# Score products of 64 rows with new turn orders, and strand work moved from VectorE to ScalarE and GpSimd

## The chip, the cores and the metric

One core of one Trainium2 chip. The metric is the device time of one launch in microseconds (us); the kernel before took 1256.9, 1262.49 and 1262.93 us in three runs, median 1262.49. A profile of one execution is given beside them. Engines: PE is TensorE (matrix products), PEld its weight loads, DVE is VectorE, ACT is ScalarE, POOL is GpSimd, SP the engine that issues most transfers.

## What is computed

A macaron block on x of 2 x 1024 tokens by 512 channels, in float32:

```python
x = x + 0.5 * ffn(layernorm(x))
x = x + attn(layernorm(x))
x = x + 0.5 * ffn(layernorm(x))

def ffn(x):            # 8 experts of rank 16, the two best of a softmax router
    h = einsum('td,erd->ter', x, lora_A)
    lora = einsum('ter,eor,te->to', h, lora_B, w_top2) * 2.0
    return x @ W_base.T + b_base + lora

def bitnet_linear(x, W, scale):
    s = maximum(mean(abs(W), axis=1), 1e-8)
    y = einsum('bsi,oi->bso', x, sign(W / s[:, None])) * (s * scale)
    return nan_to_num(y, nan=0.0, posinf=1e6, neginf=-1e6)

def attn(x):           # 32 query heads, 8 key/value heads, head width 16
    q, k, v = (bitnet_linear(x, W, sc) for W, sc in ((Wq, qs), (Wk, ks), (Wv, vs)))
    p = softmax(q @ k.T / 4)          # each key/value head serves 4 query heads
    return bitnet_linear(p @ v, Wo, os)
```

## The kernel before

**Layout.** Tokens are cut into tiles of 128; four tiles are a group, so there are groups (b, g) = (0,0), (0,1), (1,0), (1,1). PSUM has eight banks of 128 x 512: seven rotate under the tag `w` (`bank`), one holds the value sums `av`.

**Units and turns.** The attention works on 32 units: batch, block of 512 queries, key/value head. A unit has 4 query heads. `attention` (L831) runs a loop of turns. In one turn stand eight score tiles for the row maxima of one unit (`m_tile`, 128 queries by 512 keys), eight score tiles for the exponentials of an earlier unit (`e_tile`, 128 keys by 512 queries) and the value products (`a_part`) of what the turn before exponentiated. A unit takes four turns in each role.

**A score tile.** Queries and keys are held as a rounded high part and a low part, so that products in the reduced format (fp32r) keep the precision of float32. The tile `q` has 32 rows for each head: 16 high, 16 low; four heads fill 128 partitions. The tile `k` holds the high and the low keys side by side, repeated on every 16 rows. A product of 32 rows against the low keys and one against the high keys are summed in a bank (L742, L781). An exponential's tile gets a third product of 2 rows, which subtracts the row maximum (L785). A product of 32 rows uses a strip of 32 of TensorE's 128 rows; head h lies on strip h.

**After the product.** VectorE reduces each m tile to its negated maximum (`m_max`, L751); ScalarE exponentiates each e tile (L787). The value products (L820) use all 128 rows and 32 columns each, so that four heads lie side by side.

**Order.** All instructions are issued in an order written out by the program, and every engine works through its own in order. A turn follows one of three texts: `FULL` when a strand has a TensorE step ready, else `BARE`; `LEAD_IN` before the first exponentials. In them `m0(5)` and `m1(5)` are the two products of m tile 5, `e0(3)`, `e1(3)` and `e2(3)` the three of e tile 3, `A0` to `A3` the four quarters of the value products, `S` the placing of a unit's maxima; `F` offers one TensorE step to the strands, `V` one VectorE operation, `C` one ScalarE operation, `W` and `D` the same under a condition. Tile i belongs to head i mod 4.

**Strands.** Everything else (first FFN, projections, output projection, second FFN) is written as Python generators which the planner `Flow` runs beside the attention. A `yield "v", "P"` asks for a VectorE slot after a TensorE step; a table of delays (`LATER`) in planner ticks, 64 to a turn, says how long after a step the next may be issued. `flow.stock` counts buffers: `t` are the temporary 128 x 512 tiles. `flow.free` is true outside the attention. Where a unit needs projections that are not issued yet, `need` (L839) issues strand steps alone, ahead of the turn's further instructions, until they are; `place(u)` (L682) then loads a unit's q and k. Unit 16 is the first of batch 1; it is placed at the end of turn 60.

**Steps that the change touches.** `finite` (L226) is nan_to_num of four elementwise operations and a predicated copy; in strands beside the attention, three run on GpSimd and the mask (L251) and the copy (L259) on VectorE. `ln_T` normalizes a tile on VectorE (L288), transposes it on TensorE and copies it on ScalarE. `base` in the FFN forms x + b/2 in a new tile on GpSimd (L414) and adds the product on VectorE (L425). `o_proj` multiplies by the output scale on VectorE (L639). `qkv_part` stores the high and low parts of queries and keys to `qd` and `kd` in DRAM (L543).

## Time and profile before

| | us |
|---|---|
| median of three runs | 1262.49 |
| the profiled execution, its own time | 1256.92 |
| its span, first to last instruction | 1255.2 |
| TensorE busy | 1148.8 |
| VectorE busy (reductions of m tiles: 657.0) | 902.8 |
| ScalarE busy (exponentials: 546.9) | 641.6 |
| GpSimd busy | 295.0 |
| mean granted TensorE clock | 0.915 |

A busy engine is one that has an instruction in it; overlapping matrix products count once, and their ends are modelled. So the starts of products tell more than their lengths. Idle time of an engine that is not the bound costs nothing. The chain of work that ended last follows the time back from the last instruction, at each step to what released it. In a line of groups or of the timeline, `out<-in` are tile names without their numbers, and `32*128 32x512` is a product on 32 rows and 128 columns of the array over 512 moving columns. A matrix product in full float32 appears as two instructions.

### The profile page before, as it was taken

How to read it: one execution, taken by the hardware profiler on the slowest of the kernel's cores; microseconds unless marked ns; L12 is line 12 of the kernel's file. 1: busy time of each engine (PE TensorE's matmuls, PEld its weight loads, DVE VectorE, ACT ScalarE, POOL GpSimd, SP SyncE). 2: the span in 40 equal slices, each digit the busy share in tenths (PEclk: the TensorE clock that was granted, in tenths of full speed). 3: DMA queues.
4: the chain of work that ended last, by engine and by line, in shares of the span. 5: the costliest groups of instructions: out<-in, count | busy, mean ns of one | idle time of the engine just before them, and what ended most of it. 6: DMA issues, size and time to landing. Idle time of an engine off the chain costs nothing.

```text
span 1255.2 us, 25499 instructions
## 1 busy us (share of the span) xinstructions
PE 1148.8 (92%) x10501; PEld 606.1 (48%) x10501; DVE 902.8 (72%) x1733; ACT 641.6 (51%) x1249; POOL 295.0 (24%) x302
## 2 busy tenths in 40 slices
PE   3988699999999999999999999999999999998868
PEld 3546355454454544444554445444455444545434
DVE  5578876767786777776677976777769677895273
ACT  2222255655554665565565666455557655566401
POOL 3135832000000340031555220241000300422110
PEclk8989588899986999987999899899989899999788
DMA  7010332121212222223132241122222422211110
GB/s 254 1 59 34 81 122 85 52 52 52 52 52 52 69 80 57 70 76 89 49 90 75 72 122 53 33 52 69 61 60 67 123 68 65 68 55 38 45 39 34
DMA packets 38708, 85.57 MB, mean 68 GB/s; under 512 B 7728, under 2 KB 10800, under 8 KB 34624
## 3 DMA queue, kind: packets, MB, share of 16 engines
q1 hardware_dynamic: 37184, 81.26, 22.4%
q8 instruction: 82, 1.34, 0.4%
q10 hardware_dynamic: 1152, 2.10, 0.4%
q0 software_dynamic: 256, 0.59, 0.3%
q14 instruction: 34, 0.28, 0.1%
HBM read 59.57 MB, written 23.84 MB: 66 GB/s over the span
## 4 chain that ended last, share of the span: by engine, by line
PE 70%; DVE 19%; issue 3%; DMA 2%; POOL 2%; ACT 1%; SPq 1%; POOLq 0%; ACTq 0%; DVEq 0%
PE av L820 20%; PE m L742 16%; DVE mn L751 11%; PE e L781 10%; PE pbf L419 5%; PE pbs L419 5%; PE e L785 4%; PE po L634 2%; PE phs L342 1%; DMA qd<-y 1%; PE pq L504 1%; PE pbf L423 1%; PE pv L521 1%; PE pbs L423 1%; DMA x<-in_x 1%
## 5 line engine op out<-in xcount | busy, mean ns | idle before, releaser
L751 DVE TENSOR_REDUCE mn<-m 128x1 f32<-128x512 f32 x1024 | 657.0, 682 | 230.0 <-PE m L742 221.4
L787 ACT ACTIVATE es<-e 128x512 f32<-128x512 f32 x1024 | 546.9, 599 | 425.6 <-PE e L785 401.4
L742 PE MATMUL m<-k,q 32*128 32x512 f32 x2048 | 492.1, 464 | 21.1 <-DVE mn L751 15.1
L781 PE MATMUL e<-q,k 32*128 32x512 f32 x2048 | 407.9, 474 | 8.3 <-DVE mn L751 6.9
L742 PEld LDWEIGHTS m<-k,q 32*128 32x128 f32 x2048 | 240.8, 196 | 153.0 <-issue 67.4
L820 PE MATMUL av<-es,vaug 128*32 128x256 f32 x4096 | 290.3, 416 | 16.4 <-issue 10.3
L781 PEld LDWEIGHTS e<-q,k 32*128 32x128 f32 x2048 | 185.1, 194 | 114.7 <-DVE mn L751 69.6
L785 PE MATMUL e<-mq,ones_r 2*128 2x512 f32 x1024 | 233.0, 431 | 3.7 <-DMA mq<-mT 3.7
L820 PEld LDWEIGHTS av<-es,vaug 128*32 128x32 f32 x4096 | 121.5, 116 | 154.5 <-issue 103.8
L785 PEld LDWEIGHTS e<-mq,ones_r 2*128 2x128 f32 x1024 | 125.6, 196 | 25.1 <-issue 13.7
L419 PE MATMUL pbf<-wb,xTf 128*128 128x512 f32 x128 | 68.9, 653 | 1.3 <-DVE mn L751 1.3
L419 PE MATMUL pbs<-wb,xTs 128*128 128x512 f32 x128 | 64.8, 618 | 1.2 <-DVE mn L751 1.2
L586 POOL TENSOR_TENSOR an<-an,rb 128x512 f32<-128x512 f32 x15 | 19.2, 1281 | 142.7 <-DMA rd<-rs 72.1
L249 POOL TENSOR_SCALAR loa<-y 128x512 f32<-128x512 f32 x17 | 12.7, 750 | 157.1 <-ACT y L509 147.5
L726 POOL MEMSET vaug<- 128x128 f32 x32 | 6.6, 206 | 137.7 <-PE av L820 137.6
L419 PEld LDWEIGHTS pbf<-wb,xTf 128*128 128x128 f32 x128 | 23.2, 203 | 30.1 <-issue 26.1
L419 PEld LDWEIGHTS pbs<-wb,xTs 128*128 128x128 f32 x128 | 21.5, 189 | 27.1 <-issue 22.9
L253 POOL TENSOR_SCALAR z<-y 128x512 f32<-128x512 f32 x17 | 34.1, 2008 | 1.8 <-DMA qd<-y 0.6
L249 POOL TENSOR_SCALAR loo<-yo 128x512 f32<-128x512 f32 x12 | 7.4, 613 | 113.7 <-DVE yo L639 110.0
L537 POOL TENSOR_TENSOR z<-z,y 128x512 fp32r<-128x512 f32 x17 | 21.9, 1293 | 51.0 <-ACT y L534 51.0
L590 POOL TENSOR_TENSOR anxL<-an,anxT 128x512 fp32r<-128x512 f32 x15 | 19.2, 1280 | 53.5 <-ACT anxT L588 53.4
L634 PE MATMUL po<-sign_o,anxT 128*128 128x512 f32 x64 | 29.4, 459 | 1.2 <-DVE mn L751 1.2
(193 smaller groups left out, 1008.3 us busy)
## 6 DMA issues: line engine op xcount, KB each, us to landing
k<-kd SPq DMA_DIRECT2D x31, 1024.0 KB
q<-qd SPq DMA_DIRECT2D x32, 256.0 KB
ad<-avs SPq DMA_DIRECT2D x32, 256.0 KB
x<-in_x SPq DMA_DIRECT2D x16, 256.0 KB
qd<-y SPq DMA_DIRECT2D x16, 256.0 KB
qd<-z SPq DMA_DIRECT2D x16, 256.0 KB
an<-ad SPq DMA_DIRECT2D x15, 256.0 KB
rb<-rd SPq DMA_DIRECT2D x15, 256.0 KB
```

The source lines that it names most:

```text
L249: nc.gpsimd.tensor_scalar(lo_, y, 0.0, -BIG, ALU.min, ALU.max)
L253: nc.gpsimd.tensor_scalar(o, y, 0.0, BIG, ALU.max, ALU.min)
L419: nc.tensor.matmul(pb, xT[:, c, t * P:(t + 1) * P], wb[:, c, :], start=(c == 0), stop=False)
L423: nc.tensor.matmul(pb, hT[0][:, t * P:(t + 1) * P], lb, start=False, stop=True)
L537: (nc.vector if fast else nc.gpsimd).tensor_tensor(lo, o, y, ALU.subtract)
L634: nc.tensor.matmul(po, hs[j][:, c, t * P:(t + 1) * P], wo[:, c, :], start=(c + j == 0), stop=(c + j == KC))
L742: nc.tensor.matmul(s["m", i], s["q"][rows, qt * P:(qt + 1) * P], s["k"][rows, 1 - p, kh * 512:(kh + 1) * 512], start=(p == 0), stop=(p == 1))
L751: nc.vector.tensor_reduce(s["mn"][:, h, qt, kh:kh + 1], s.pop(("m", i)), AX.X, ALU.max, negate=True)
L781: nc.tensor.matmul(t, s["k"][rows, 1 - p, kt * P:(kt + 1) * P], s["q"][rows, :], start=(p == 0), stop=False)
L785: nc.tensor.matmul(t, ones_r[two, :], s["mq"][two, :], start=False, stop=True)
L787: nc.scalar.activation(e, s.pop(("e", i)), AF.Exp, scale=HD ** -0.5)
L820: nc.tensor.matmul(s["av"][32 * h:32 * h + 32, cols], s["v"][:, kt, :], s["es"][kt * REP + h][:, cols], start=(kt + half == 0), stop=(kt + ...
```

## The change

- The q and k of a unit now lie in one tile. The keys are stored as 64 rows for each key/value head (high twice, low twice) and loaded to both halves of the partitions; the queries' 32 rows are loaded twice, so that one product of 64 rows gives the whole score. An m tile takes one product instead of two, an e tile two (64 rows and 2 rows) instead of three. Heads 0 and 1 lie on partitions 0 to 63, heads 2 and 3 on 64 to 127.
- The three turn texts are new. `e1` is now the 2-row product. The choice between FULL and BARE looks ahead to the place of the first `F`.
- Before a unit's first value product, the planner now waits until the copy of the unit before has been issued.
- In strands beside the attention: the normalization runs on ScalarE with a bias that GpSimd computes; the mask of `finite` on GpSimd; the FFN's sum as a scaled copy on ScalarE and an addition on GpSimd; the output scale as a copy on ScalarE and a product on GpSimd. x + b/2 is formed in place. Outside the attention these stay on VectorE.
- 13 temporary tiles instead of 11 (stock 12 for 10).

```diff
     p2 = ctx.enter_context(tc.tile_pool(name="p2", bufs=2))
-    tmp = ctx.enter_context(tc.tile_pool(name="tmp", bufs=11))
+    tmp = ctx.enter_context(tc.tile_pool(name="tmp", bufs=13))
     sm = ctx.enter_context(tc.tile_pool(name="sm", bufs=4))
...
             self.t, self.free, self.strands, self.n = 0, True, [], 0
-            self.stock = dict(m=3, n=4, t=10, xT=2, xL=2, hT=1, fb=6)
+            self.stock = dict(m=3, n=4, t=12, xT=2, xL=2, hT=1, fb=6)
             self.lock = None
...
             nc.gpsimd.tensor_scalar(lo_, y, 0.0, -BIG, ALU.min, ALU.max)
-            yield "v", src, t
-            nc.vector.tensor_scalar(m_, y, 0.0, 0.0, ALU.mult, ALU.is_equal)
+            yield "g", ""
+            nc.gpsimd.tensor_scalar(m_, y, 0.0, 0.0, ALU.mult, ALU.is_equal)
             yield "g", ""
...
         nc.gpsimd.tensor_tensor(rstd[:, own], ve[:, own], mhalf[:, own], ALU.pow)
+        calm = not flow.free
+        if calm:
+            yield "g", ""
+            neg = sm.tile([P, TG], F32, tag="neg", name=f"neg{n}{tiles[0]}", bufs=4)
+            nc.gpsimd.tensor_tensor(neg[:, own], mv[:, own, 0], rstd[:, own], ALU.mult)
+            yield "g", ""
+            nc.gpsimd.tensor_scalar(neg[:, own], neg[:, own], -1.0, None, ALU.mult)
         at = flow.t
...
             yield "r", dict(t=1)
-            yield "v", "g", at
+            yield "a" if calm else "v", "g", at
             xn = t512(f"xn{n}_{t}")
-            nc.vector.tensor_scalar(xn, xt[:, t, :], mv[:, t, 0:1], rstd[:, t:t + 1], ALU.subtract,
-                                    ALU.mult)
-            yield "P", "v", None, 1
+            if calm:
+                nc.scalar.activation(xn, xt[:, t, :], AF.Identity, bias=neg[:, t:t + 1],
+                                     scale=rstd[:, t:t + 1])
+            else:
+                nc.vector.tensor_scalar(xn, xt[:, t, :], mv[:, t, 0:1], rstd[:, t:t + 1],
+                                        ALU.subtract, ALU.mult)
+            yield "P", "a" if calm else "v", None, 1
             pt = bank(f"pt{n}_{t}").rearrange("p (c q) -> p c q", c=KC)
...
             yield "g", ""
-            xb = t512(f"xb{n}_{t}")
-            nc.gpsimd.tensor_tensor(xb, xt[:, t, :], bh, ALU.add)
+            nc.gpsimd.tensor_tensor(xt[:, t, :], xt[:, t, :], bh, ALU.add)
             for c in range(KC):
...
             nc.tensor.matmul(pb, hT[0][:, t * P:(t + 1) * P], lb, start=False, stop=True)
-            yield "v", "P"
-            nc.vector.scalar_tensor_tensor(xt[:, t, :], pb, 0.5, xb, ALU.mult, ALU.add)
-            flow.give(t=1, fb=1)
+            if flow.free:
+                yield "v", "P"
+                nc.vector.scalar_tensor_tensor(xt[:, t, :], pb, 0.5, xt[:, t, :], ALU.mult, ALU.add)
+                flow.give(t=1, fb=1)
+            else:
+                yield "a", "P"
+                hb = t512(f"hb{n}_{t}")
+                nc.scalar.activation(hb, pb, AF.Copy, scale=0.5)
+                flow.give(fb=1)
+                yield "g", "a"
+                nc.gpsimd.tensor_tensor(xt[:, t, :], xt[:, t, :], hb, ALU.add)
+                flow.give(t=1)
             if store is not None:
-                yield ("a" if flow.free else "d"), "v"
+                yield ("a" if flow.free else "d"), "v" if flow.free else "g"
                 (nc.scalar if flow.free else nc.sync).dma_start(store[t * P:(t + 1) * P, :],
...
             if mv2 is not None:
-                yield "v", "v"
+                yield "v", "v" if flow.free else "g"
                 stats(xt, t, mv2, n)
...
             for j, t in enumerate((y, o)):
-                dst = (qd[b][i * 2 * P:(i + 1) * 2 * P, cols].rearrange(
-                           "(h i d) s -> h i d s", i=2, d=HD)[:, j, :, :] if i < KC
-                       else kd[b][:, j * S + g * GT:j * S + (g + 1) * GT])
-                yield ("d", "v" if fast else "g") if j == 0 else ("d", "d")
-                nc.sync.dma_start(dst, t)
+                n_ = 2 if i < KC else 4
+                dst = (qd[b][i * 2 * P:(i + 1) * 2 * P, cols] if i < KC else kd[b][:, cols]).rearrange(
+                    "(h i d) s -> h i d s", i=n_, d=HD)
+                for c in range(n_ // 2):
+                    yield ("d", "v" if fast else "g") if j + c == 0 else ("d", "d")
+                    nc.sync.dma_start(dst[:, j * n_ // 2 + c, :, :], t)
         flow.give(t=2 if i <= KC else 1)
...
                 flow.lock = ss[t] if c < 2 else None
-            yield "v", "P"
+            yield "v" if fast else "a", "P"
             y = t512(f"yo{n}_{t}")
-            nc.vector.tensor_tensor(y, po, osc, ALU.mult)
+            if fast:
+                nc.vector.tensor_tensor(y, po, osc, ALU.mult)
+            else:
+                nc.scalar.copy(y, po)
             flow.give(fb=1)
             done.append(t)
+            if not fast:
+                yield "g", "a"
+                nc.gpsimd.tensor_tensor(y, y, osc, ALU.mult)
             r = t512(f"ro{n}_{t}")
-            yield from finite(y[:, :], r[:, :], f"o{n}_{t}", fast, ("v", flow.t))
+            yield from finite(y[:, :], r[:, :], f"o{n}_{t}", fast, ("v" if fast else "g", flow.t))
             yield "v" if fast else "g", "v"
...
-    FULL = ("e0(3) e0(2) m0(5) m0(0) e1(3) e1(2) m1(5) V m1(0) e2(3) e2(2) C e0(1) A0 A1 A2 A3 S "
-            "m0(1) m0(6) e0(7) e0(4) m1(1) m1(6) e1(7) W e1(4) e1(1) m0(2) e2(7) e2(4) e2(1) C "
-            "m1(2) V F e0(6) e0(0) m0(7) e0(5) e1(6) e1(0) m1(7) e1(5) e2(6) e2(0) D m0(3) e2(5) "
-            "m0(4) m1(3) F m1(4)")
-    BARE = ("C m0(1) m0(2) e0(3) e0(4) V m1(1) e0(6) e1(3) e1(4) m0(5) e1(6) e2(4) e2(3) m1(5) "
-            "m1(2) A0 S e2(6) e0(1) m0(0) e0(7) e1(1) C m1(0) e1(7) W m0(6) e2(1) e0(0) e2(7) m1(6) "
-            "A1 e1(0) V m0(7) e0(5) e0(2) e2(0) D m1(7) e1(2) e1(5) m0(4) m0(3) e2(2) e2(5) m1(4) "
-            "m1(3) A2 A3")
-    LEAD_IN = ("m0(0) m0(5) m0(2) V m1(0) m1(5) F C V m0(7) m1(2) m1(7) V F C m0(4) m0(1) m0(6) V m1(4) "
-               "m1(1) F C V m0(3) V m1(6) S m1(3) F C V")
+    FULL = ("m0(5) V m0(3) C F F e0(4) m0(7) V W e0(1) e0(3) e1(1) e1(4) e0(2) e1(2) e1(3) m0(1) C "
+            "A0 A1 S e0(6) e0(0) e1(6) e0(5) m0(6) e1(0) e1(5) m0(2) D A2 A3 m0(4) e0(7) m0(0) "
+            "e1(7)")
+    BARE = ("e0(0) W m0(2) A0 S C e0(3) e1(0) e0(2) m0(4) e1(2) e1(3) m0(1) A1 A2 m0(0) C m0(7) "
+            "e0(1) e0(6) e0(4) e1(6) e1(4) D e1(1) m0(6) A3 m0(5) V e0(7) e0(5) m0(3) e1(5) e1(7) V")
+    LEAD_IN = ("m0(0) m0(5) m0(2) V m0(7) F C V m0(4) m0(1) V F C m0(6) V F C V m0(3) V S F C V")
     FULL, BARE, LEAD_IN = (
...
          for o in t.split()] for t in (FULL, BARE, LEAD_IN))
+    at_F = TICK * FULL.index(("F", 0, 0)) // len(FULL)
     TU = NT // 2
...
         b, qb, g = units[u]
-        q = p2.tile([P, 512], F32R, tag="q", name=f"q{u}", bufs=3)
-        nc.sync.dma_start(q.bitcast(F32), qd[b][g * P:(g + 1) * P, qb * 512:(qb + 1) * 512])
-        k = p2.tile([P, 2, S], F32R, tag="k", name=f"k{u}", bufs=3)
+        qk = p2.tile([P, 2, S], F32R, tag="k", name=f"k{u}", bufs=3)
+        q, k = qk[:, 0, :].rearrange("p (t s) -> p t s", t=2), qk[:, 1, :]
         st[u].update(q=q, k=k, es={}, mq=p2.tile([P, 512], F32R, tag="mq", name=f"mq{u}", bufs=3),
                      mn=p2.tile([P, REP, 4, 2], F32, tag="mn", name=f"mn{u}"))
+        for t in range(2):
+            for h in range(2):
+                row = g * P + (2 * h + t) * 32
+                nc.sync.dma_start(q.bitcast(F32)[64 * h:64 * h + 64, t, :],
+                                  qd[b][row:row + 32, qb * 512:(qb + 1) * 512].unsqueeze(0)
+                                  .to_broadcast([2, 32, 512]))
         if u:
-            nc.sync.dma_start(k.bitcast(F32).rearrange("p i s -> p (i s)"),
-                              kd[b][g * HD:(g + 1) * HD, :].unsqueeze(0).to_broadcast(
-                                  [P // HD, HD, 2 * S]))
-
-    def place_k(half):
-
-        for i in range(2):
-            nc.sync.dma_start(st[0]["k"].bitcast(F32)[:, i, half * 512:(half + 1) * 512],
-                              kd[0][0:HD, i * S + half * 512:i * S + (half + 1) * 512]
-                              .unsqueeze(0).to_broadcast([P // HD, HD, 512]))
+            place_k(u, 0, S)
+
+    def place_k(u, s0, s1):
+        b, _, g = units[u]
+        nc.sync.dma_start(st[u]["k"].bitcast(F32)[:, s0:s1],
+                          kd[b][g * 64:(g + 1) * 64, s0:s1].unsqueeze(0).to_broadcast(
+                              [2, 64, s1 - s0]))
...
         place(0)
-        place_k(0)
+        place_k(0, 0, 512)
         for j in range(4):
             yield "P", "d" if j == 0 else "", None, 4
-            for p in range(2):
-                for h in range(REP):
-                    m_tile(0, j * REP + h, p, False)
+            for h in range(REP):
+                m_tile(0, j * REP + h, False)
             for h in range(REP):
...
         yield "d", "x"
-        place_k(1)
+        place_k(0, 512, S)
...
-    def m_tile(u, i, p, end=True):
+    def rows_of(h):
+        return slice(64 * (h // 2), 64 * (h // 2) + 64)
+
+    def m_tile(u, i, end=True):
...
         h, (qt, kh) = i % REP, m_where(u, i)
-        rows = slice(32 * h, 32 * h + 32)
-        if p == 0:
-            s["m", i] = bank(f"m{u}_{i}")
-        nc.tensor.matmul(s["m", i], s["q"][rows, qt * P:(qt + 1) * P],
-                         s["k"][rows, 1 - p, kh * 512:(kh + 1) * 512],
-                         start=(p == 0), stop=(p == 1))
-        if p == 1 and end:
+        s["m", i] = bank(f"m{u}_{i}")
+        nc.tensor.matmul(s["m", i], s["q"][rows_of(h), h % 2, qt * P:(qt + 1) * P],
+                         s["k"][rows_of(h), kh * 512:(kh + 1) * 512], start=True, stop=True)
+        if end:
             m_max(u, i)
...
         kt, h = i // REP, i % REP
-        rows = slice(32 * h, 32 * h + 32)
         if p == 0:
-            s["e", i] = bank(f"e{u}_{i}")
-        t = s["e", i]
-        if p < 2:
-            nc.tensor.matmul(t, s["k"][rows, 1 - p, kt * P:(kt + 1) * P], s["q"][rows, :],
-                             start=(p == 0), stop=False)
+            t = s["e", i] = bank(f"e{u}_{i}")
+            nc.tensor.matmul(t, s["k"][rows_of(h), kt * P:(kt + 1) * P], s["q"][rows_of(h), h % 2, :],
+                             start=True, stop=False)
         else:
+            t = s["e", i]
             two = slice(32 * h, 32 * h + 2)
...
         def need(*keys):
+            until(lambda: set(keys) <= ended)
+
+        def until(cond):
             for _ in range(4000):
                 flow.settle()
-                if set(keys) <= ended:
+                if cond():
                     return
...
                 place_v(e[0])
-            order = (LEAD_IN if not e and not a else FULL if flow.wants("P", begin + TICK * 5 // 8)
+            order = (LEAD_IN if not e and not a else FULL if flow.wants("P", begin + at_F)
                      else BARE)
...
                     if m:
-                        m_tile(m[0], m[1] * 2 * REP + i, p)
+                        m_tile(m[0], m[1] * 2 * REP + i)
                 elif kind == "e":
...
                     if a:
+                        if a[0] and a[1] == p == 0:
+                            until(lambda: "av" not in st[a[0] - 1])
                         a_part(a[0], a[1] * 2 + p // 2, p % 2)
...
     qd = [dram.tile([2 * D, S], F32, tag="qd", name=f"qd{b}") for b in range(B)]
-    kd = [dram.tile([P, 2 * S], F32, tag="kd", name=f"kd{b}") for b in range(B)]
+    kd = [dram.tile([4 * P, S], F32, tag="kd", name=f"kd{b}") for b in range(B)]
     ad = [dram.tile([G * P, S], F32, tag="ad", name=f"ad{b}") for b in range(B)]
...
     rd = [dram.tile([NQB, H, 512], F32, tag="rd", name=f"rd{b}") for b in range(B)]

```

## The prediction

> **What bounds the kernel now.** I read the page first (engine totals, then the chain that ended last), then the waits, then stretches of the timeline of TensorE, VectorE and GpSimd inside the attention, and last the order of the instructions in the two programs.
>
> ```profile
> span 1255.2 us, 25499 instructions
> PE 1148.8 (92%) x10501; PEld 606.1 (48%) x10501; DVE 902.8 (72%) x1733; ACT 641.6 (51%) x1249; POOL 295.0 (24%) x302
> ...
> PE 70%; DVE 19%; issue 3%; DMA 2%; POOL 2%; ACT 1%; SPq 1%; POOLq 0%; ACTq 0%; DVEq 0%
> ```
>
> TensorE is the bound, VectorE the second. One full turn of the attention, from TensorE's timeline, with its columns start, length, engine, line, operation, tiles, shapes, count:
>
> ```profile
> 893.53 0.50 PE L742 MATMUL m<-k,q 32*128 32x512 f32 x2
> 893.54 0.49 PE L781 MATMUL e<-q,k 32*128 32x512 f32 x2
> 893.87 0.39 PE L742 MATMUL m<-k,q 32*128 32x512 f32 x1
> 893.87 0.39 PE L781 MATMUL e<-q,k 32*128 32x512 f32 x2
> 894.10 0.38 PE L781 MATMUL e<-q,k 32*128 32x512 f32 x1
> 894.11 0.40 PE L785 MATMUL e<-mq,ones_r 2*128 2x512 f32 x2
> 894.33 0.39 PE L785 MATMUL e<-mq,ones_r 2*128 2x512 f32 x1
> 894.66 1.13 PE L419 MATMUL pbs<-wb,xTs 128*128 128x512 f32 x2
> 895.71 0.50 PE L781 MATMUL e<-q,k 32*128 32x512 f32 x2
> ...
> 899.00 1.93 PE L820 MATMUL av<-es,vaug 128*32 128x256 f32 x32
> ```
>
> Starts are what counts. Four products on four different strips of 32 rows start within 0.01 us; the next four 0.23 us later (893.87, 894.10, 894.33). I call such a step a slot. Where the shape changes, a step is longer: 894.33 to 894.66 is 0.33 before the 128-row product, and the second slot after the change comes 0.34 after the first (893.53 to 893.87). So a change of shape costs about 0.1 on either side, 0.2 in all. The busy time of stretches (us; PE, PEld, DVE, ACT, POOL) gives the two kinds of turn:
>
> ```profile
> 891.67:899.00 7.33, 7.33 (x81) 3.49 (x77) 5.03 (x9) 4.24 (x8) 0.00 (x0) 1.00 0.13 41
> 708.95:714.55 5.60, 5.60 (x74) 2.87 (x72) 5.53 (x12) 4.33 (x9) 0.00 (x0) 1.00 0.01 3
> ```
>
> A FULL turn (two strand steps in it) is TensorE's: 7.33 of 7.33, VectorE 5.03. A BARE turn is VectorE's: eight reductions of 0.61 us pitch ("706.95 4.86 DVE" for eight, below) and any strand operation between them make 5.53 of 5.60.
>
> ```profile
> 706.95 4.86 DVE L751 TENSOR_REDUCE mn<-m 128x1 f32<-128x512 f32 x8
> ```
>
> The program holds 97 FULL and 32 BARE turns before, 94 and 35 after.
>
> **The score products.** Before, a turn has 16 + 16 products of 32 rows and 8 of 2 rows, 40 strips, 10 slots of four; its orders need 11. After, it has 8 + 8 of 64 rows (two strips each) and 8 of 2 rows: again 40 strips. Packing the new FULL by hand (heads 0 and 1 on the lower half, 2 and 3 on the upper, a 2-row product on the head's own strip): m4+e7, m0+e1(7), m5+m3, then the two strand steps, e4+m7, e1+e3, e1(1)+e1(4)+e2, e1(2)+e1(3)+m1, A0 A1, e6+e0, e1(6)+e5, m6+e1(0)+e1(5), m2, A2 A3: 11 slots. BARE packs into 11 too. Changes between score, strand and value products are six per FULL turn in both. Halving the products saves no array time by itself. What can shrink is the slot, 0.233 with four weight loads, towards the 0.216 of the value products (32 starts in eight steps): nothing to 11 x 0.017 = 0.19 a FULL turn. Half of that, 94 x 0.1: **-9**.
>
> **The open price: 64-row and 2-row products side by side.** In the new orders the shapes alternate inside a group. No row shows a 64-row product. From below: nothing, as at 893.87 to 894.33, where 2-row products follow 32-row ones on the same strip at 0.23 and start beside them within 0.01. From above: the 0.2 of the 32-to-128 change, and no overlap across shapes. FULL then has 10 changes (around e1(1) e1(4); e1(2) e1(3); e1(6); e1(0) e1(5); e1(7)) and 14 slots for 11: 10 x 0.2 + 3 x 0.233 = 2.7 us. BARE has 8 changes and 14 slots: 2.3, less 0.3 that VectorE covers. I take the lower end, because in every change that costs, one side is 128 rows or crosses all strips and must wait for all of them, while both sides here stay on strips, like the 2/32 pair. The upper end stays in the range.
>
> The Trainium skill's TensorEngine Tiling (Array Packing), Key Properties, says that changing the tiling mode, not just the tile, drains the engine, and lists 64-row and 32-row tiling as different modes. The 0.33 and 0.34 steps above agree with it for 32 to 128 rows; no run here shows 64 to 32. By that rule the sum would take the upper end.
>
> **Earlier banks.** A max tile holds its bank for one product instead of two that lie slots apart. TensorE sat idle behind "DVE mn L751" for 15.1 us at line 742 and 6.9 at 781. Bounds 0 to -22, a third: **-7**.
>
> **VectorE's load.** Removed beside the attention: 28 normalizations (12 x 0.755 + 8 x 0.603 + 8 x 0.538 = 18.2 us), 33 masks (10.3 + 8.1 + 4 x 0.49 = 20.4), 12 output scales (x 0.676 = 8.1), 20 sums (x 0.685 = 13.7): 60 us of 903. The chain has VectorE at 19%, 10.9% of it reductions; the other 8.1% is 102 us of the 246 us that are not reductions, 41%. 60 x 0.41: **-25**. Bounds: 0, where the new engine is waited for as long, and -60.
>
> **ScalarE and GpSimd take it.** ScalarE gets 60 operations of 0.60 us, 36 us, hidden in a FULL turn (4.24 of 7.33); in a BARE turn 4.33 + 2 x 0.6 reaches 5.53. Nothing, at most +8. GpSimd gets 12 scales and 20 sums of 1.28 (41 us) and 33 masks between 0.61 (line 249) and 1.92 (line 253), both two-step operations on the same tile; 1.3 taken, 43 us. 295 + 84 of 1255 is no bound overall, but at two places GpSimd is in the path.
>
> First, batch 1's query, key and value parts. Unit 16 needs them issued, and before turn 61 the planner stops the attention's instructions until they are. GpSimd and VectorE there, before:
>
> ```profile
> 634.83 0.61 POOL L249 TENSOR_SCALAR loa<-y 128x512 f32<-128x512 f32 x1
> 635.52 1.97 POOL L253 TENSOR_SCALAR z<-y 128x512 f32<-128x512 f32 x1
> 637.57 1.27 POOL L255 TENSOR_TENSOR z<-z,loa 128x512 f32<-128x512 f32 x1
> ...
> 633.89 0.73 DVE L259 COPY_PREDICATED z<-ma,y 128x512 f32<-128x512 uint8 x1 [1.23 <-POOL z L255]
> ```
>
> Before, the six predicated copies of group (1,1) stand in VectorE's order with 3 to 14 instructions between them. After, they stand in a row, ahead of turn 61's reductions, and each waits for its four GpSimd operations. A part takes 0.69 + 2.05 + 1.3 (starts above) + a mask of 1.3 = 5.4 us; six, 32 us (28 to 36). TensorE has five more parts of eight products at 0.235, 9.4 us, and some 3 us of turn 61 until its banks wait for the reductions. The idle is 32 - 9.4 - 3 = 20 us, where 2 are idle now: **+18** (+8 to +24).
>
> Second, the start: between 94 and 164 us GpSimd is busy 44.5 of 70 us and in the chain; some eight masks join it, 10 us, of which VectorE gives back 5 (59.5 of 70 busy): **+4** (0 to +8).
>
> **The rest.** A0 moves to the head of BARE, four slots behind the last value product of the old unit, whose bank ScalarE must copy first (0.60 us, behind exponentials): nine units begin so, 0.3 each, **+3** (0 to +8). SP issues 407 transfers for 303 (a unit's q in four pieces, one k; the key's stores doubled), and a unit's load falls from 1280 to 1024 KB; SP's longest waits are for work, not for its queue: 0 (0 to +3). With seven strands left instead of ten the end has 48 strand steps on TensorE for 57: **-1** (0 to -4). In-place bias sums move nothing.
>
> Sum: -9 - 7 - 25 + 18 + 4 + 3 - 1 = -17 on the profiled execution's 1256.9 (span 1255.2 and 1.7 around it; the median of the three is 1262.5, 0.4% above): **1240 us**. Own range 1205 to 1275.
>
> **Rivals.**
> - *Shapes drain everywhere* (the other side): in every turn, inside the score groups. For it: the same 0.33 at every change of shape that the trace has. Against: 2 and 32 rows mix freely. Price 94 x 2.7 + 35 x 2.0 = 324, so 1564; at 0.1 a change, 94 x 1.7 + 35 x 1.2 = 202, so 1442. It decides at once if the shapes never overlap, for three lost slots a turn are 3 x 0.233 x 129 = 90 us; if they do overlap, from 0.014 us a change (17 over 1220 changes).
> - *Only the half that changes waits*: five changes in the fuller half of either order, 94 x 1.0 + 35 x 0.7 = 119: 1359.
> - *GpSimd takes the gain back*: its masks at 1.92 and the path share of VectorE's strands passed on to its helpers: turn 61 at +24, the start +8, relief -5: 1240 + 6 + 4 + 20 = 1270. For it: "PE 70%" leaves strands little to give. Against: GpSimd is idle for three quarters.
>
> **How the numbers follow.** Shapes free 0.57, in which GpSimd takes it back 0.12; one half waits 0.13; drains everywhere 0.30. The measurement tells 0.5%. Faster 0.42, same 0.08 (0.05 of the third rival, 0.03 of the forecast's case), slower 0.07 + 0.13 + 0.30 = 0.50. The range: from 1208 (a tenth of the forecast's case below it) to 1545, which takes in the second rival and most of the first; some 0.15 is left out.
>
> **What would show it.** Right: in TensorE's timeline a 2-row and a 64-row product starting together, steps of 0.22 to 0.23 within a group, FULL turns of 7.1 to 7.3; about 850 us of VectorE; one idle stretch of TensorE near turn 61 with six predicated copies released by GpSimd. Wrong: steps of 0.33 and more inside the score groups and turns of 8 to 10 us; or masks near 2 us on GpSimd and VectorE waiting for "POOL z" throughout.

## The result, and the profile after

The changed kernel takes 1715.5 us (median of four runs, 1686.5 to 1719.4; a fifth took 1709.9) against 1261.5 for the kernel before on the same chip: 1.347 times as long, 95% interval 1.330 to 1.364. Ratios and intervals, here and below, come from the fast runs alone (of the changed kernel 1686.5 and 1709.9), so they are not quotients of the medians. The forecast was 1240, the range 1208 to 1545. Direction, size and range were wrong. The profiled execution of the changed kernel is the fastest of the four (1686.5, span 1684.7); its span is 429.5 us longer than that of before.

The page of the changed kernel: span, engine totals, granted clock in 40 slices, and the chain that ended last, by engine and by line.

```profile
span 1684.7 us, 21759 instructions
...
PE 1560.4 (93%) x8453; PEld 708.3 (42%) x8453; DVE 881.5 (52%) x1642; ACT 688.0 (41%) x1307; POOL 398.1 (24%) x381
...
PEclk8985669999989799777685576999656979996998
...
PE 83%; DVE 6%; POOL 3%; DMA 3%; issue 2%; ACT 1%; SPq 0%; DVEq 0%; POOLq 0%; ACTq 0%
PE av L842 19%; PE e L802 17%; PE e L807 17%; PE m L767 16%; PE pbs L429 3%; PE pbf L429 3%; DVE mn L775 2%; PE po L654 2%; DMA qd<-y 1%; PE phs L353 1%; PE pq L523 1%; POOL ma L251 1%; DMA k<-kd 1%; PE pbs L433 1%; DMA x<-in_x 1%
```

TensorE issues 2048 products fewer and is busy 412 us longer. It holds 83% of the chain instead of 70, and the 2-row product, 4% before, holds 17%. Why is in TensorE's timeline (start, length, engine, line, operation, tiles, shapes, count):

```profile
1009.52 0.64 PE L842 MATMUL av<-es,vaug 128*32 128x256 f32 x8
1010.09 0.49 PE L767 MATMUL m<-k 64*128 64x512 f32 x1
1010.09 0.72 PE L802 MATMUL e<-k 64*128 64x512 f32 x2
1010.43 0.39 PE L767 MATMUL m<-k 64*128 64x512 f32 x1
1010.75 0.50 PE L807 MATMUL e<-mq,ones_r 2*128 2x512 f32 x2
1011.18 0.49 PE L802 MATMUL e<-k 64*128 64x512 f32 x1
1011.18 0.49 PE L767 MATMUL m<-k 64*128 64x512 f32 x1
1011.60 0.64 PE L842 MATMUL av<-es,vaug 128*32 128x256 f32 x8
1012.17 0.50 PE L802 MATMUL e<-k 64*128 64x512 f32 x1
1012.60 0.50 PE L807 MATMUL e<-mq,ones_r 2*128 2x512 f32 x1
1013.03 0.50 PE L802 MATMUL e<-k 64*128 64x512 f32 x1
1013.03 0.50 PE L767 MATMUL m<-k 64*128 64x512 f32 x1
```

Two 64-row products on different halves start together (1010.09, 1011.18, 1013.03). A 2-row product never starts beside a 64-row one, whatever strip it is on: of the 1195 places in the trace where the two follow each other, none has them start within 0.1 us. A slot that stands between two changes of height takes 0.43 (1010.75 to 1011.18; 1012.17 to 1012.60 to 1013.03) where one among its own height takes 0.23: the same 0.1 on either side of a change as from 32 to 128 rows before. By stretch (PE, PEld, DVE, ACT, POOL, clock, DMA share, GB/s) a FULL and a BARE turn are now

```profile
1008.77:1018.72 9.95, 9.95 (x74) 4.11 (x74) 9.03 (x25) 6.52 (x13) 1.28 (x1) 1.00 0.09 31
1506.68:1514.23 7.55, 7.55 (x57) 3.17 (x57) 5.88 (x12) 3.26 (x6) 3.56 (x4) 1.00 0.22 85
```

With nothing else to wait for, FULL takes 9.95 us at full clock (7.35 before), BARE 7.55 (5.6). With the program's 94 and 35 turns that is 94 x 2.6 + 35 x 1.95 = 313 us. The other 117 are the start, 28 later at the first value product (191.4 us; 163.7 before), less 4 at the end, and 93 more inside the attention: 18 of new idle at turn 61, and 75 that are left to a lower clock, less waits that fall away. The clock records of the trace have half clock for 509 us of the attention, 140 before. At half clock a FULL turn takes 15.3 to 15.9 us and a BARE turn 13.1 to 14.2; so 369 us more of it cost between 369 x (1 - 9.95/15.3) = 129 and 369 x (1 - 7.55/14.2) = 173, an estimate. What falls away are the waits for VectorE of the kernel before: its turns at full clock took 7.64 on average, where 97 of 7.35 and 32 of 5.6 would give 6.92.

### The profile page after: what moved, and what is told of

It is laid out like the page before. It is cut to its first block, busy times and chain, and to the rows that moved or that the text cites. A ratio compares the mean times of both kernels' runs of the same rounds, so it can differ in the third digit from the quotient of the medians.

```text
span 1684.7 us, 21759 instructions
## 1 busy us (share of the span) xinstructions
PE 1560.4 (93%) x8453; PEld 708.3 (42%) x8453; DVE 881.5 (52%) x1642; ACT 688.0 (41%) x1307; POOL 398.1 (24%) x381
## 4 chain that ended last, share of the span: by engine, by line
PE 83%; DVE 6%; POOL 3%; DMA 3%; issue 2%; ACT 1%; SPq 0%; DVEq 0%; POOLq 0%; ACTq 0%
PE av L842 19%; PE e L802 17%; PE e L807 17%; PE m L767 16%; PE pbs L429 3%; PE pbf L429 3%; DVE mn L775 2%; PE po L654 2%; DMA qd<-y 1%; PE phs L353 1%; PE pq L523 1%; POOL ma L251 1%; DMA k<-kd 1%; PE pbs L433 1%; DMA x<-in_x 1%
## 5 line engine op out<-in xcount | busy, mean ns | idle before, releaser
L775 DVE TENSOR_REDUCE mn<-m 128x1 f32<-128x512 f32 x1024 | 678.1, 686 | 628.6 <-PE m L767 512.8
L767 PE MATMUL m<-k 64*128 64x512 f32 x1024 | 474.4, 566 | 33.7 <-DMA k<-kd 16.0
L802 PE MATMUL e<-k 64*128 64x512 f32 x1024 | 408.9, 533 | 27.4 <-ACT es L809 24.1
L842 PE MATMUL av<-es,vaug 128*32 128x256 f32 x4096 | 339.6, 451 | 10.3 <-issue 10.3
L807 PE MATMUL e<-mq,ones_r 2*128 2x512 f32 x1024 | 339.3, 563 | 0.0
L767 PEld LDWEIGHTS m<-k 64*128 64x128 f32 x1024 | 179.5, 215 | 225.4 <-issue 147.4
L802 PEld LDWEIGHTS e<-k 64*128 64x128 f32 x1024 | 163.6, 216 | 208.4 <-issue 92.6
L424 POOL TENSOR_TENSOR x<-x,bh 128x512 f32<-128x512 f32 x32 | 40.9, 1298 | 28.2 <-ACT xns L296 28.2
L444 POOL TENSOR_TENSOR x<-x,hbs 128x512 f32<-128x512 f32 x10 | 12.7, 1273 | 140.0 <-ACT hbs L441 140.0
L249 POOL TENSOR_SCALAR loa<-y 128x512 f32<-128x512 f32 x17 | 13.9, 820 | 110.2 <-ACT y L528 109.4
L553 ACT CAST y<-z 128x512 fp32r<-128x512 f32 x20 | 12.5, 624 | 67.2 <-DVE z L259 65.8
L429 PEld LDWEIGHTS pbf<-wb,xTf 128*128 128x128 f32 x128 | 24.6, 205 | 28.3 <-issue 26.4
L610 POOL TENSOR_TENSOR anxL<-an,anxT 128x512 fp32r<-128x512 f32 x15 | 18.9, 1270 | 73.0 <-ACT anxT L608 73.0
```

The source lines that it names most:

```text
L424: nc.gpsimd.tensor_tensor(xt[:, t, :], xt[:, t, :], bh, ALU.add)
L429: nc.tensor.matmul(pb, xT[:, c, t * P:(t + 1) * P], wb[:, c, :], start=(c == 0), stop=False)
L444: nc.gpsimd.tensor_tensor(xt[:, t, :], xt[:, t, :], hb, ALU.add)
L767: nc.tensor.matmul(s["m", i], s["q"][rows_of(h), h % 2, qt * P:(qt + 1) * P], s["k"][rows_of(h), kh * 512:(kh + 1) * 512], start=True, sto ...
L775: nc.vector.tensor_reduce(s["mn"][:, h, qt, kh:kh + 1], s.pop(("m", i)), AX.X, ALU.max, negate=True)
L802: nc.tensor.matmul(t, s["k"][rows_of(h), kt * P:(kt + 1) * P], s["q"][rows_of(h), h % 2, :], start=True, stop=False)
```

## The experiments

Every run stood beside runs of the kernel before on the same chip (medians 1260.2 to 1260.6). Theory: a change of height inside the score groups costs as much as a change to 128 rows, and nothing overlaps across it. Rivals: 64-row products are slow themselves; the strands' move or the new orders do it.

**1. The 2-row products grouped.** The changed kernel, with the 2-row products of a turn behind all 64-row ones of a group.

```diff
-    FULL = ("m0(5) V m0(3) C F F e0(4) m0(7) V W e0(1) e0(3) e1(1) e1(4) e0(2) e1(2) e1(3) m0(1) C "
-            "A0 A1 S e0(6) e0(0) e1(6) e0(5) m0(6) e1(0) e1(5) m0(2) D A2 A3 m0(4) e0(7) m0(0) "
-            "e1(7)")
+    FULL = ("m0(5) V m0(3) C F F e0(4) m0(7) V W e0(1) e0(3) e0(2) m0(1) e1(1) e1(4) e1(2) e1(3) C "
+            "A0 A1 S e0(6) e0(0) e0(5) m0(6) e0(7) m0(4) e1(6) e1(0) e1(5) e1(7) D A2 A3 m0(0) "
+            "m0(2)")
...
```

> The changed kernel with new FULL and BARE texts in which each group's 2-row products stand together behind its 64-row products: 2 changes of shape inside a turn's score groups instead of 8 to 10, 10 slots. Theory (each change between the 64-row and the 2-row shape drains TensorE, about 0.2 us and no overlap, and the thinned stream also loses granted clock): FULL turns of about 7.5 us and BARE of 5.9 at full clock, 95 x 7.5 + 34 x 5.9 = 913 against 97 x 7.33 + 32 x 5.6 = 890 before, with the stall at turn 61 of 18 and less VectorE work about 1270 us (1240 to 1310), mean clock back above 0.89. Rival (64-row products are slow, or cost clock, by themselves): above 1600, clock near 0.82. Rival (the strands' work on GpSimd and ScalarE is what costs): above 1600 too.

Measured: 1435.3, ratio 1.138 (1.132 to 1.144). The median turn at full clock takes 8.23; 229 us of the attention are at half clock. The order alone takes 280 us off, which points at the alternation; runs 2 and 6 test it with the orders kept. It missed the expected 1270 by 165 us, and only part of that is seen: 27 us of idle at turn 61 instead of 20, and weight loads of 64-row products that wait 228 us in all behind VectorE and ScalarE, 164 in the changed kernel.

**2. One height for all score products.** The changed kernel and its orders; the third product written over 64 rows, zero but for two (GpSimd clears each unit's tile of maxima for it).

```diff
-            two = slice(32 * h, 32 * h + 2)
-            nc.tensor.matmul(t, ones_r[two, :], s["mq"][two, :], start=False, stop=True)
+            nc.tensor.matmul(t, sel_r[rows_of(h), h % 2, :], s["mq"][rows_of(h), :], start=False,
+                             stop=True)
```

> The changed kernel with its own turn texts, but the maximum is subtracted by a product of 64 rows (zero weights on the rows that are not the head's), so that all score products have one shape. No change inside a score group, but the third product fills half of the array instead of a quarter: 13 slots a FULL turn instead of 11. Theory: steps of 0.23 inside the groups, FULL about 7.7 us, BARE about 6.0, in all about 1295 us (1250 to 1330), clock above 0.89. Rival (64-row products slow by themselves): more of them, so 1690 or above. Rival (strands): about 1690.

Measured: 1334.0, ratio 1.058 (1.052 to 1.063); a median turn of 7.50, half clock for 154 us. TensorE's timeline in this run, the same products in the same order:

```profile
715.26 0.50 PE L807 MATMUL e<-k 64*128 64x512 f32 x1
715.26 0.50 PE L811 MATMUL e<-mq,sel_r 64*128 64x512 f32 x1
715.59 0.39 PE L807 MATMUL e<-k 64*128 64x512 f32 x1
715.60 0.39 PE L772 MATMUL m<-k 64*128 64x512 f32 x1
715.83 0.39 PE L811 MATMUL e<-mq,sel_r 64*128 64x512 f32 x1
715.83 0.39 PE L772 MATMUL m<-k 64*128 64x512 f32 x1
716.06 0.39 PE L811 MATMUL e<-mq,sel_r 64*128 64x512 f32 x1
```

More rows are multiplied and 382 us are saved: products of one height start side by side and follow at 0.23 (715.60, 715.83, 716.06). Neither the 64-row product nor the order is slow. The time lies 4 us above the expected range. With TensorE faster, the key load of experiment 7 is no longer hidden: TensorE waits for keys 13 times in this run, 44 us in all, where the changed kernel waits twice, 16 us.

**3 and 4. Each part of the change alone.** 3 is the kernel before with only the strands' part of the change; 4 is the changed kernel with that part undone (it keeps the 13 temporary tiles and the planner's wait). Of run 3 the mask's edit, which experiment 5 takes back:

```diff
-            yield "v", src, t
-            nc.vector.tensor_scalar(m_, y, 0.0, 0.0, ALU.mult, ALU.is_equal)
+            yield "g", ""
+            nc.gpsimd.tensor_scalar(m_, y, 0.0, 0.0, ALU.mult, ALU.is_equal)
```

> The kernel before with only the strands' part of the change (normalization, sums, scales and masks on ScalarE and GpSimd; 11 temporary tiles as before; the planner's wait before a unit's first value product). Theory (the strands cost little): the prediction's terms for them, -25 for VectorE's load, +18 at turn 61, +4 at the start, so about 1255 us (1235 to 1280), with an idle stretch of TensorE of 10 to 20 us near turn 61. Rival (the strands carry the loss): above 1500.

> The changed kernel with the strands' work put back on VectorE: 64-row products, the new turn texts, nothing else. Theory (change of shape): the whole loss stays, about 1680 us (1640 to 1710), turns of 9.95 and 7.5 us at full clock; with TensorE slower than VectorE the removed relief is worth nothing. Rival (strands): near 1260.

Measured: strands only 1275.7, ratio 1.012 (1.005 to 1.020); scores only 1705.7 (1.353; 1.343 to 1.364). So the whole of the loss lies in the score part, as run 4 was to show. Run 3 lost 15 us where the middle of its expectation was a gain of 5, though it stays within the range given.

**5. The strands' part without the masks.** Run 3 with the mask line left on VectorE; normalizations, sums and scales still moved.

> The kernel before with the strands' normalizations, FFN sums and output scales moved off VectorE beside the attention as in the change, and the masks left on VectorE; the score products as before. The run with the masks moved too took 1275.7 (+1.2 per cent) with 13.8 us of idle near turn 61 and a start 3.3 us later. If VectorE's relief is worth what the prediction put on it (40 of the 60 us are these three: 40 x 0.41 = 16), 1245 (1235 to 1252). If ScalarE and GpSimd hand the same waits on and the relief is worth nothing, 1260 (1255 to 1266), and the loss of the other run lies in the masks alone.

Measured: 1238.7, ratio 0.987 (0.981 to 0.993): 21.5 us faster than before by the medians, 8 to 24 by the interval. The masks alone cost 1275.7 - 1238.7 = 37 us by the medians, 32 by the ratios. In run 3 TensorE idles 13.8 us near turn 61 and VectorE waits 24.6 us for GpSimd:

```profile
DVE z L259 <- POOL z L255: 24.6, 6, 7.1
```

Without the moved masks that idle is gone, the first value product starts at 163.4 instead of 167.0, and half clock in the attention is 96 us instead of 151.

**6. The suspected cause alone, in the kernel before.** Its own orders and 32-row products; the third product has another height (and two cleared tiles hold the maxima, for three).

```diff
-            two = slice(32 * h, 32 * h + 2)
-            nc.tensor.matmul(t, ones_r[two, :], s["mq"][two, :], start=False, stop=True)
+            two = slice(64 * (h // 2), 64 * (h // 2) + 64)
+            nc.tensor.matmul(t, sel_r[two, h % 2, :], s["mq"][two, :], start=False, stop=True)
```

> The kernel before with its own orders and its own 32-row products, and one thing changed: the third product of each exponential tile (the maximum) is written over 64 rows, 62 of them zero, instead of over 2. The shapes now alternate inside the score groups as in the changed kernel. Counted from the orders: a FULL turn has 8 more changes of shape and 18 slots instead of 12, a BARE turn 11 more and 18 instead of 11. If a change of tile height drains the array (0.1 us on either side, and nothing runs side by side across it): FULL 8 x 0.2 + 6 x 0.233 = +3.0, BARE 11 x 0.2 + 7 x 0.233 - 0.3 = +3.5, together 97 x 3.0 + 32 x 3.5 = 403, so 1663, and up to 150 more if the granted clock follows the alternation as it did in the changed kernel. If heights mix freely and the new orders of the changed kernel were at fault, only the 8 more strips count: 2 slots x 0.233 x 129 = 60, so 1320.

Measured: 1648.0, ratio 1.298 (1.286 to 1.310); expected 1663. One FULL turn by stretch, and four rows of it:

```profile
556.67:566.95 10.28, 10.28 (x77) 4.50 (x76) 5.88 (x10) 4.71 (x11) 0.00 (x0) 1.00 0.51 148
```

```profile
562.23 0.50 PE L792 MATMUL e<-mq,sel_r 64*128 64x512 f32 x2
562.66 0.49 PE L749 MATMUL m<-k,q 32*128 32x512 f32 x1
563.08 0.49 PE L792 MATMUL e<-mq,sel_r 64*128 64x512 f32 x1
563.50 0.50 PE L749 MATMUL m<-k,q 32*128 32x512 f32 x2
```

The median turn at full clock is 10.29; the count of changes and slots gave 7.35 + 3.0 = 10.35 for FULL. BARE turns take 9.05 for 9.1. Steps of 0.42 to 0.43 again, now between 64 and 32 rows. This settles the cause: a 64-row product runs beside neither a 32-row one (here) nor a 2-row one (in the changed kernel), and each change costs the same. That the total comes so near is partly luck: the count holds neither the half clock, 307 us of the attention here and 140 before, nor the waits of before that fall away.

**7. The key load.** In the changed kernel the first value product starts 28 us later than before, and while a unit's 512 KB of queries and 512 KB of keys come in, the transfers run at 50 GB/s (149 to 172 us). Run 7 loads the keys as two plain loads of 64 rows.

```diff
-        nc.sync.dma_start(st[u]["k"].bitcast(F32)[:, s0:s1],
-                          kd[b][g * 64:(g + 1) * 64, s0:s1].unsqueeze(0).to_broadcast(
-                              [2, 64, s1 - s0]))
+        for a in range(2):
+            nc.sync.dma_start(st[u]["k"].bitcast(F32)[64 * a:64 * a + 64, s0:s1],
+                              kd[b][g * 64:(g + 1) * 64, s0:s1])
```

> The changed kernel, and the key load of a unit as two plain loads of 64 rows in place of one that repeats 64 rows twice; the same bytes. In the changed kernel that load moves 512 KB in about 20 us (149 to 170 us) at 50 GB/s and about 11 per cent of the 16 DMA engines, in the kernel before 2 MB move at 145 GB/s and 50 per cent (131 to 145 us); and the first value product starts at 191.4 us instead of 163.7. If the repeat of two is what makes the load slow (two engines of sixteen), the loads go as fast as before or faster, the start gains 20 to 28 us and the later loads stay hidden: 1715 - 25 = 1690 (1670 to 1700). If it is the number and size of rows, nothing changes: 1715. The turns stay at 9.95 and 7.55 us at full clock either way.

Measured: 1681.7, ratio 1.333 (1.321 to 1.345); the interval overlaps that of the changed kernel. The first value product starts at 179.0, so 12 of the 28 us are back. The expectation had put the whole 20 us down to the 512 KB of keys; the queries' loads, as large, repeat twice as well and kept some 47 to 53 GB/s here. The pair of runs 9 and 10 tells it cleanly.

**8 to 11. One product for each score tile.** If one height is what matters, the maximum can ride in the same product. The queries' rows become high, low, high and two rows of the maximum, the keys' high, high, low and ones: 48 rows for the maxima's pass, 50 for the exponentials' (the two start side by side, in run 11 for instance both at 737.53). The low-by-low part is left out. The queries are loaded plainly, in pieces of 32 and 16 rows.

```diff
-        if p == 0:
-            t = s["e", i] = bank(f"e{u}_{i}")
-            nc.tensor.matmul(t, s["k"][rows_of(h), kt * P:(kt + 1) * P], s["q"][rows_of(h), h % 2, :],
-                             start=True, stop=False)
-        else:
...
+        t = bank(f"e{u}_{i}")
+        nc.tensor.matmul(t, s["k"][rows_of(h, 2), kt * P:(kt + 1) * P],
+                         s["q"][rows_of(h, 2), h % 2, :], start=True, stop=True)
...
+    FULL = ("m0(0) e0(2) V e0(0) m0(2) C F F m0(1) e0(3) W e0(1) m0(3) V C A0 A1 S m0(4) e0(6) "
+            "e0(4) m0(6) D A2 A3 m0(5) e0(7) e0(5) m0(7)")
+    BARE = ("m0(0) e0(2) W e0(0) m0(2) C A0 S A1 m0(1) e0(3) e0(1) m0(3) C V A2 A3 m0(4) e0(6) D "
+            "e0(4) m0(6) V m0(5) e0(7) e0(5) m0(7)")
```

Run 8 is that in the changed kernel; 9 puts the masks back on VectorE (the edit of run 3, reversed); 10 also loads the keys as in run 7; 11 also puts normalizations, sums and scales back.

> The changed kernel with one product per score tile: the rows of the key stand as high, high, low, ones and those of the query as high, low, high and two rows of the maximum, 48 rows for the maximum's pass and 50 for the exponential's. It leaves out the low-by-low part of the score product (part of the computation changed, so the time is for three of four partial products). All score products have one shape, and a turn has 16 of them (8 slots of two) for the 24 (11 slots) before. If what costs in the changed kernel is the change of shape alone, this is the run with one shape for all score products less three slots a turn: 1334 - 129 x 3 x 0.23 = 1245, less what the banks free earlier give, up to 40: 1205 to 1250. If a 64-row product itself is slow (two that share a slot run one after the other), a turn stays over 9 us and the time over 1450. If VectorE is the bound by then (eight reductions and a strand operation, 5.5 us), 1250 to 1270.

> The same with one product per score tile (the low-by-low part left out too), and the mask of `finite` back on VectorE as in the kernel before. If the six parts before turn 61 wait for GpSimd, the idle of 20 us there falls to 9 to 14 (a part's GpSimd time goes from 6.4 to 4.0 us, six parts), and the start gains about 4: 10 to 18 us under the run with the masks on GpSimd. If VectorE is the bound in the turns, 33 masks x 0.62 = 20 us come back there, and the two are equal.

> The same as the last (one product per score tile without the low-by-low part, masks on VectorE), and the key load as two plain loads of 64 rows. If the repeat of two makes the load slow, the start gains 20 to 28 us and idle stretches that end at a key load in later units go too: 20 to 60 us under the run before it in this list. If not: the same time.

> One product per score tile (without the low-by-low part), two plain key loads, masks on VectorE, and also the normalizations, sums and output scales back on VectorE as in the kernel before: the score part of the change in its other form, without any of its strand part. Against the run that differs only in these three on ScalarE and GpSimd (1156.6): there the chain has VectorE's reductions at 14.3 per cent, and a turn is 7.0 us with 5.5 of VectorE. If the relief is worth something where VectorE is nearer to being the bound, 40 x 0.4 = 16 us slower: 1172 (1165 to 1185). If it is worth nothing: 1157, or some us less, as the strands then take no hop over GpSimd.

| run | us | ratio, 95% interval |
|---|---|---|
| 8 one product | 1186.7 | 0.941 (0.938 to 0.945) |
| 9 and masks on VectorE | 1177.4 | 0.935 (0.931 to 0.940) |
| 10 and plain key loads | 1156.6 | 0.917 (0.913 to 0.921) |
| 11 and all strands as before | 1139.1 | 0.905 (0.901 to 0.909) |

Run 8 beat its expectation by 18 us. The masks are worth 9.4 (expected 10 to 18; the two intervals overlap): TensorE's longest idle in the middle of the run goes from 20.3 to 3.7 us. The key load is worth 20.7 (expected 20 to 60). The same 512 KB, in runs 9 and 10, in 40 slices from 140 to 162 us (share of the DMA engines in tenths, GB/s):

```profile
DMA  3101111111111111111110000000000000000001
GB/s 60 15 0 60 30 45 60 45 60 45 60 45 60 52 52 60 45 60 45 60 45 15 0 0 0 0 0 0 0 0 0 0 0 0 0 0 0 15 15 37
```

```profile
DMA  3789910000000000000000000000000153666896
GB/s 60 112 268 305 238 30 0 0 0 0 0 0 0 0 0 0 0 0 0 0 0 0 0 0 0 0 0 0 0 15 15 30 52 48 194 235 156 212 261 209
```

With the repeat of two it takes 11 us at some 50 GB/s, with a tenth of the engines; plainly 3 us at up to 305.

Run 11 went against its expectation: with the strands back on VectorE it gains 17.5 us more, where moving them off VectorE gained 21.5 in run 5. Run 11 has 905 us from the first to the last value product, run 10 922; turns of 6.84 and 6.93 on average at full clock, 74 and 91 us of half clock. Why the sign turns was not tested. Run 11 is the fastest version, 9.5% below the kernel before, with the low-by-low part left out. A full turn of it by stretch, and the page's chain:

```profile
734.87:741.83 6.96, 6.65 (x55) 2.84 (x53) 6.39 (x12) 4.77 (x10) 2.87 (x2) 1.00 0.33 92
```

```profile
PE 61%; DVE 27%; DMA 4%; issue 3%; ACT 2%; POOL 2%; SPq 1%; DVEq 0%; ACTq 0%; POOLq 0%
```

VectorE is busy for 6.39 of 6.96 us: the two engines are close to even.

## Why the prediction was wrong

**The failed step** is "The open price: 64-row and 2-row products side by side". It took "the lower end, because in every change that costs, one side is 128 rows or crosses all strips and must wait for all of them, while both sides here stay on strips, like the 2/32 pair". The runs show another rule: 2 and 32 rows run side by side, and so do 48 and 50, but 64 rows run with neither 2 nor 32, even on separate strips. The upper end was right to a tenth: 10 changes and three lost slots were priced at 2.7 for FULL and 2.0 for BARE; 2.6 and 1.95 were measured. The same counting gave run 6 to 0.06 us a turn. The Trainium skill's TensorEngine Tiling (Array Packing), Key Properties, which the prediction cited and set aside, agrees with runs 2 and 6.

**Chances.** The rival "Shapes drain everywhere", which had the mechanism, was given 0.30 and 1442 to 1564; 2 and 32 rows were the only mixed pair in the trace, and it could not separate "stays on strips" from "same kind of height". Slower had 0.50 in all and faster 0.42, so the forecast of a gain was not the likelier side even by its own chances. The rival missed the time too, since both it and the range left out the next two points.

**Not in the sum: the granted clock.** No term or rival had it. By the estimate above it costs 129 to 173 us before the waits that fall away, some 75 net. From the rival's 1564 to the profiled 1686.5 that leaves the start (28 where 4 stood) and the gains of 9, 7 and 25 that the sum had taken off and that turns bound by TensorE do not show: 75 + 24 + 41, less 17 in smaller terms.

**"Transfers 0 (0 to +3)"** was wrong. It counted issues and bytes and not the form of the transfer; SP's waits said nothing about the engines behind it. 12 us came back in run 7, 20.7 in the step from run 9 to 10. The Trainium skill has the rule that was not applied, in DMA: Bandwidth & Descriptors, Rules for kernel authors: a transfer uses no more engines than the count of its outermost dimension, so a leading repeat of c copies keeps it on at most c. The rows agree: 11.4% of 16 engines is 1.8 with a repeat of two (149 to 172 us), and the 50.2% of before is 8.0 with a repeat of eight (131 to 145 us, with a query load and a store beside it).

**"The score products", -9.** Half the weight loads were to shorten the slot of 0.233 towards 0.216. Two 64-row products a slot follow at 0.23 (run 2): nothing.

**"VectorE's load", -25** was right in kind: run 5, with 40 of the 60 us, gained 21.5 (8 to 24) where its share of the term was 16. In run 3 the masks took more than it brought, and in the changed kernel, whose turns are TensorE's, none of it shows (1.347 with the strands' part, 1.353 without). **"ScalarE and GpSimd take it"**: the stall at turn 61 was priced at +18 and measured 19.85 idle where 2 were; the reasons hold row by row (stretch of the idle, then GpSimd's and VectorE's timeline):

```profile
790.80:810.80 20.00, 0.15 (x3) 0.04 (x1) 2.18 (x3) 2.44 (x5) 19.11 (x13) 0.56 0.09 26
```

```profile
795.84 1.12 POOL L249 TENSOR_SCALAR loa<-y 128x512 f32<-128x512 f32 x1
797.02 1.93 POOL L251 TENSOR_SCALAR ma<-y 128x512 uint8<-128x512 f32 x1
799.01 1.92 POOL L253 TENSOR_SCALAR z<-y 128x512 f32<-128x512 f32 x1
```

```profile
795.79 0.73 DVE L259 COPY_PREDICATED z<-ma,y 128x512 f32<-128x512 uint8 x1 [5.81 <-POOL z L255]
802.31 0.73 DVE L259 COPY_PREDICATED z<-ma,y 128x512 f32<-128x512 uint8 x1 [5.79 <-POOL z L255]
808.83 0.73 DVE L259 COPY_PREDICATED z<-ma,y 128x512 f32<-128x512 uint8 x1 [5.79 <-POOL z L255]
```

The copies stand in a row, each behind its GpSimd operations, at a pitch of 6.5 us for the 5.4 forecast. The mask took 1.93, the upper of its two rows, where 1.3 was taken, and the clamp before it 1.12 where the row had 0.61. Six parts at 6.5 less the 12.4 of cover would be 27, so some 7 us more must have been covered than was counted, by what was not followed up. The total came out right by luck, with two errors in it. The start's +4 measured 3.3 in run 3.

**The small terms.** The +3 for A0 behind the copy of the old unit did not come: TensorE's waits there add up to 12.0 us before and 10.3 after. The end is 4 us shorter for the -1 forecast, inside its range. **"Earlier banks", -7,** can't be read off the changed kernel, where TensorE sits 4.5 us behind the reductions in all (22 before). Runs 8 to 11, which hold a bank for one product, are consistent with a gain but change more than that.

## What to carry to other kernels

Before a matrix product gets another number of rows, write down the sequence of heights that TensorE will see and count the changes (here between 128, 64 and at most 32 rows): each costs about 0.2 us and ends all side-by-side running, and padding a product with zeros to the height of its neighbours is far cheaper. When work is taken off an engine, price each moved operation on its new engine by the upper row, and look for the place where the program waits for the new chain in one piece. A transfer is judged by its form as well as its bytes: a source repeated twice took 11 us where two plain loads took 3.

## What the runs showed of the hardware that was not expected

- Half clock is granted more where heights alternate, but not by their count. In the attention it is granted for 140 us of 1022 before, 154 of 1086 in run 2 and 74 of 905 in run 11, whose score products all run side by side; for 229 of 1181 in run 1, 509 of 1427 in the changed kernel and 611 of 1448 in run 4; and for 307 of 1414 in run 6, which alternates about as often as the changed kernel. Most of it lies around BARE turns, which have no strand products: from a FULL turn's value products to those of a FULL turn next to it, 203 of 868 us are at half clock in the changed kernel and 58 of 821 in run 6, in the rest of the attention 306 of 559 and 249 of 593. TensorE has work throughout, as the longest stretch in the changed kernel shows (columns as above):

```profile
868.00:984.00 116.00, 114.97 (x479) 47.19 (x478) 49.05 (x84) 40.72 (x74) 5.99 (x10) 0.50 0.11 38
```

  The Trainium skill's TensorE: Matmul & The Clock Gate, Part 1, has the half clock follow a window of idleness, in one kernel frequent short ones; here the trace has TensorE idle for 1.0 of 116 us, so the rule as worded does not cover it. What makes the chip lower the clock was not tested; the figures are all that is shown.
- On GpSimd the mask (multiply, compare) of a 128 x 512 tile takes 1.93 us in the rows above, and the clamp before it (L249) 1.12 there and 0.61 in the row of before, both two-step operations.
